# The last image's depthwise stage in another written-out order: TensorE's three parts first, VectorE's last part at the end

## The chip, the cores and the metric

The kernel runs on one NeuronCore of a Trainium2 chip. The metric is the device time of one execution in microseconds (us); smaller is better. All data are float32.

## The reference, cut to what matters

Four images of 256 channels and 64x64 pixels pass through four layers, each with a normalisation before it and a residual sum after it. The change touches only layer 2, and in it only the work of the last image: a small network generates, for each image, a 3x3 filter for every channel (`dk`) and a 256x256 mixing matrix (`pk`); the filters are applied channel by channel (depthwise), and the matrix mixes the channels (pointwise).

```python
def _gen_kernel(x, W1, b1, W2, b2):
    h = jax.nn.relu(jnp.einsum('bchw,rc->brhw', x, W1) + b1[None, :, None, None])
    pooled = h.mean(axis=(2, 3))
    return pooled @ W2.T + b2
B, C, H, W = x.shape
dk = _gen_kernel(x, Wd1, bd1, Wd2, bd2).reshape(B, C, K, K)
pk = _gen_kernel(x, Wp1, bp1, Wp2, bp2).reshape(B, O, C)
dw = lax.conv_general_dilated(x.reshape(1, B * C, H, W), dk.reshape(B * C, 1, K, K), (1, 1),
                              [(1, 1), (1, 1)], feature_group_count=B * C, ...).reshape(B, C, Ho, Wo)
out = jnp.einsum('bchw,boc->bohw', dw, pk) + bias[None, :, None, None]
...
x = x + _L2_conv_ref(_gn(x), ...)      # layer 2
x = x + _L3_conv_ref(_gn(x), ...)      # layer 3 follows
```

## The kernel before, in words

**Layout.** The 256 channels are two halves (`h` = 0 and 1, `NH` = 2) of 128 partitions; an image is `big[:, h, 4096 pixels]`. The normalised input of layer 2 lies in `xp` with a row of zeros above and below (`xin` is its inside). The depthwise result is made in eight parts: `PARTS` lists (c, h) for four stretches `c` of 1024 pixels and two channel halves, so part `2c + h` is half `h` of stretch `c`.

**Two ways to make a part.** On VectorE, ScalarE first writes the centre tap (`centre`, L1290), and then eight scalar_tensor_tensor instructions of 128x1024 add the other taps (`taps`, recorded at the helper's line L127). On TensorE, `taps_by_products` (matmul at L1339) multiplies the shifted input by nine diagonal matrices (`diag`, which ScalarE makes at L1352 from the filters of half 1). A part takes two PSUM banks of 512 columns, nine products each; after the ninth product ScalarE copies the bank to the part's tile (L1342). A float32 product appears in the trace as two matmul records. The images before the last make all eight parts on VectorE; only the last image has `diag`, because only there nothing of another image's attention is left for TensorE to do beside it.

**The mixing matrix.** `pk` starts as a bias and takes R = 8 scalar_tensor_tensor steps of 128x512, one for each slice of `wp2`. A DMA of SP's queue (`load_wp2`, L1223) brings two slices into one tile of the `k4` pool, so there are four loads.

**Pointwise.** For a stretch `c` and each 512 columns `s` of it, four products (two output halves `oh`, two input halves `h`, L1298) go to two PSUM banks; `pointwise_added` adds each bank to `big` on VectorE with a running sum (L1310), and ScalarE squares the result for the next layer's statistics (L1312). PSUM has eight banks of one pool, given out in turn (`bank`).

**Order.** The program is scheduled by hand: every engine executes its instructions in the order in which the Python code issues them, and a semaphore wait at an instruction holds what is behind it on the same engine. `Chain.later(n, f)` puts off a piece of work by n steps of the generator; `tick` runs what is due. `Chain.fill(n)` issues matmuls (L1444) of n pieces of the image before, which were kept in `held`; `Chain.settle()` issues their additions on VectorE (`res`, L127) and their stores (L1450, SP).

For the last image the order before the change is: VectorE makes the parts 0, 1, 2, 4, 6 (`mine`), TensorE the parts 3, 5, 7 (`others`). A credit lets TensorE's products in beside VectorE's taps, 54 products over 40 taps. After part 0 come `settle` and the eight steps of `pk`; two of the four slice loads are issued ahead, the other two after the second and the fourth step. The pointwise products of a stretch are put off by one and two steps after its last part on VectorE. `run(last)` runs this chain alone: no attention of another image is beside it.

The layer that follows (`mixed`) needs the sums of the whole image, so it begins with a wait for the last `pointwise_added`; its experts' load (L1390) is the next DMA in SP's order.

Of the kernel before, what the change touches and what calls it, by code (L numbers as in the profile page):

```python
# [10 lines left out]
ALU = mybir.AluOpType  # L11
# [3 lines left out]
NH = 2  # L15
HW = 64
N = HW * HW
CH = 1024
# [3 lines left out]
R = 8  # L22
# [71 lines left out]
def conv_preact_fast(ctx: ExitStack, tc: tile.TileContext, guard, x, wc, wtpg, ww, wqkv, wout, w1cat, wd2,  # L94
# [11 lines left out]
    def k4(name):  # L106
        return wk.tile([P, CH], F32, tag="k4", name=name, bufs=9)
# [3 lines left out]
    def k2(name):  # L111
        return wk.tile([P, 512], F32, tag="k2", name=name, bufs=5)
# [4 lines left out]
    def junk():  # L117
        return wk.tile([P, 512], F32, tag="junk", name="junk")

    def bank(name):  # L120
        return pp.tile([P, 512], F32, tag="bank", name=name, bufs=8)

    def tt(o, a, b, op):
        nc.vector.tensor_tensor(o, a, b, op)  # L124

    def stt(o, a, s, b, op0, op1):
        nc.vector.scalar_tensor_tensor(o, a, s, b, op0, op1)  # L127
# [119 lines left out]
    taps = wc_s.rearrange("p h (i j) o -> p h i (j o)", i=3)  # L247
# [950 lines left out]
    def generated(w, b, big, k4, st, sh, diag):  # L1198
# [19 lines left out]
        pk = k2("pk")  # L1218
        nc.sync.dma_start(out=pk, in_=bp2)

        def load_wp2(j):
            t = pool4("wp2").rearrange("p (r o) -> p r o", r=2)
            nc.sync.dma_start(out=t, in_=wp2[:, bass.ts(j, 2), :])  # L1223
            return t
# [12 lines left out]
        for c in range(N // 512):  # L1237
            if c < NC3:
                hidden(c)
            h, q = c % 2, c // 2  # L1240
# [17 lines left out]
        pb = sp.tile([P, 2 * R], F32, name="pb")  # L1258
# [25 lines left out]
        PARTS = [(c, h) for c in range(N // CH) for h in range(NH)]  # L1284

        def centre(i):
            c, h = PARTS[i]
            t = k4("dw")
            k = h * 9 + 4
            nc.scalar.activation(t.rearrange("p (y x) -> p y x", x=HW), xin[:, h, bass.ts(c, rows), :], AF.Copy, scale=dk[:, k:k + 1])  # L1290
            return t

        def pointwise(c, s, dw):
            res = []
            for oh in range(NH):
                ps = bank("ps_pw")
                for h in range(NH):
                    nc.tensor.matmul(ps, pk[:, h * NH * P + oh * P:h * NH * P + (oh + 1) * P], dw[h][:, bass.ts(s, 512)],  # L1298
                                     start=(h == 0), stop=(h == NH - 1))
                res.append(ps)  # L1300
            w.later(1, lambda: pointwise_added(2 * c + s, res))

        def pointwise_added(c, res):
            cols = bass.ts(c, 512)
            for oh in range(NH):
                if diag is None:
                    tt(big[:, oh, cols], res[oh], big[:, oh, cols], ALU.add)
                    nc.vector.bn_stats(st[:, oh, c, :], big[:, oh, cols])
                else:
                    nc.vector.scalar_tensor_tensor(big[:, oh, cols], res[oh], 1.0, big[:, oh, cols], ALU.mult, ALU.add,  # L1310
                                                   accum_out=sums[:, 0, oh, c:c + 1])
                    nc.scalar.activation(junk(), big[:, oh, cols], AF.Square, bias=pivot[:, oh:oh + 1],  # L1312
                                         accum_out=sums[:, 1, oh, c:c + 1])

        def taps(i):

            c, h = PARTS[i]
            dst = dw[i].rearrange("p (y x) -> p y x", x=HW)
            for ty, tx in TAPS:
                dx = tx - 1  # L1320
                x0, x1 = max(0, -dx), min(HW, HW - dx)
                k = h * 9 + 3 * ty + tx
                stt(dst[:, :, x0:x1], xp[:, h, c * rows + ty:c * rows + ty + rows, x0 + dx:x1 + dx], dk[:, k:k + 1],
                    dst[:, :, x0:x1], ALU.mult, ALU.add)
                yield 0.62

        def taps_by_products(parts):

            for i in parts:
                c, h = PARTS[i]  # L1330
                dw[i] = k4("dw")
                for s in range(2):
                    ps = bank("ps_dw")
                    dst = ps.rearrange("p (y x) -> p y x", x=HW)
                    for n, (ty, tx) in enumerate([(1, 1)] + TAPS):
                        dx = tx - 1
                        x0, x1 = max(0, -dx), min(HW, HW - dx)
                        y0 = (2 * c + s) * RB + ty
                        nc.tensor.matmul(dst[:, :, x0:x1], diag[:, 3 * ty + tx, :], xp[:, h, y0:y0 + RB, x0 + dx:x1 + dx],  # L1339
                                         start=(n == 0), stop=(n == 8))  # L1340
                        if n == 8:
                            nc.scalar.copy(dw[i][:, bass.ts(s, 512)], ps)  # L1342
                        yield


        mine = [i for i, (c, h) in enumerate(PARTS) if diag is None or h == 0 or c == 0]
        others = [i for i in range(len(PARTS)) if i not in mine]
        products, credit = taps_by_products(others), 0.0
        dw = {mine[0]: centre(mine[0])}
        if diag is not None:  # L1350
            for k in range(9):
                nc.scalar.activation(diag[:, k, :], ident, AF.Copy, scale=dk[:, 9 + k:10 + k])  # L1352
        slices = [load_wp2(0), load_wp2(1)]
        for n, i in enumerate(mine):
            if n + 1 < len(mine):
                dw[mine[n + 1]] = centre(mine[n + 1])
            for wait in taps(i):

                credit += 18 * len(others) / (8 * len(mine))
                while credit >= 1:  # L1360
                    credit -= 1
                    next(products, None)
                yield wait
            if n == 0:
                w.settle()
                for j in range(R):
                    stt(pk, slices[j // 2][:, j % 2, :], pb[:, R + j:R + j + 1], pk, ALU.mult, ALU.add)
                    if j % 2 == 1 and j // 2 + 2 < R // 2:
                        slices.append(load_wp2(j // 2 + 2))
                    yield 0.35  # L1370
            c, h = PARTS[i]
            if h == NH - 1 or i + 1 not in mine:
                if n == len(mine) - 1:
                    for _ in products:
                        pass
                d = [dw[2 * c + h] for h in range(NH)]
                for s in range(2):
                    w.later(1 + s, lambda c=c, s=s, d=d: pointwise(c, s, d))
        yield 2
        yield from w.pending()  # L1380
        sh2 = sp.tile([P, NH], F32, name="sh2")
        tt(sh2, sh, vec_s[:, V_L2B, :], ALU.add)
        return st, sh2
# [96 lines left out]
    def tail(b, big, qT, k4=k4, diag=None, xs_in=None, held=None):  # L1480

        def layers(w):
            st, sh = yield from nonlocal_out(w, b, big, k4, xs_in)
            st = yield from linear_attention(w, b, big, qT, k4, st, sh, diag is not None)
            st, sh = yield from generated(w, b, big, k4, st, sh, diag)
            if b + 2 < B:
                load_x(b + 2)
            elif b + 2 == B:
                for h in range(NH):
                    for q in range(2):  # L1490
                        half_image = bass.ts(q, N // 2)
                        nc.sync.dma_start(out=x_cols[:, h, half_image], in_=xs_d[b + 1, h, :, half_image])
            yield from mixed(w, b, big, k4, st, sh, held)
        return layers
# [23 lines left out]
    with tc.manual_schedule(engines={E.PE, E.Activation, E.DVE, E.Pool, E.SP}):  # L1518
# [15 lines left out]
        diag = tpg[:, NH, 0:9 * P].rearrange("p (k q) -> p k q", k=9)  # L1534
# [602 lines left out]
```

## Time and profile before

| what | value |
|---|---|
| median of 3 runs | 3113.34 us (3112.62 to 3114.3) |
| the profiled execution's own time | 3113.69 us |
| its span in the trace | 3111.8 us |
| busy: TensorE matmul, VectorE, ScalarE | 97%, 68%, 38% of the span |
| the last image's depthwise stage | 2974.6 us (first tap) to 3062.3 us (last sum) of the span |
| TensorE's work in it | 54 diagonal products and 32 pointwise products |
| VectorE's work in it | 40 taps, 8 steps of `pk`, 4 additions of `res`, 16 pointwise additions |

Times in the trace count from the span's start. "PE" is TensorE, "DVE" VectorE, "ACT" ScalarE, "SP" the engine that issues most DMAs. The shares over the whole span say little here: the change lies in a stage of 88 us, under 3% of the span, and has to be read from that stretch alone.

### The profile page before, as it was taken

How to read it: one execution, taken by the hardware profiler on the slowest of the kernel's cores; microseconds unless marked ns; L12 is line 12 of the kernel's file. 1: busy time of each engine (PE TensorE's matmuls, PEld its weight loads, DVE VectorE, ACT ScalarE, POOL GpSimd, SP SyncE). 2: the span in 40 equal slices, each digit the busy share in tenths (PEclk: the TensorE clock that was granted, in tenths of full speed). 3: DMA queues.
4: the chain of work that ended last, by engine and by line, in shares of the span. 5: the costliest groups of instructions: out<-in, count | busy, mean ns of one | idle time of the engine just before them, and what ended most of it. 6: DMA issues, size and time to landing. Idle time of an engine off the chain costs nothing.

```text
span 3111.8 us, 24418 instructions
## 1 busy us (share of the span) xinstructions
PE 3006.8 (97%) x8606; PEld 1486.8 (48%) x8606; DVE 2109.5 (68%) x2713; ACT 1174.0 (38%) x2188; POOL 131.1 (4%) x178
## 2 busy tenths in 40 slices
PE   6899999999999999999999999999999999998888
PEld 3454555445554444444565444444545544444633
DVE  8747777853557986786537896778363668864485
ACT  2134333353555322223364532222445443335621
POOL 0100000000110000000011000000100100000100
PEclk9999999999999999999999999999999999998999
DMA  5233111022101023113300102310420010111011
GB/s 217 77 105 137 35 51 30 31 55 85 40 11 34 7 75 125 39 43 63 109 11 1 41 21 82 107 46 29 102 75 1 11 34 14 44 49 63 14 61 65
DMA packets 58913, 174.25 MB, mean 56 GB/s; under 512 B 6432, under 2 KB 16416, under 8 KB 54560
## 3 DMA queue, kind: packets, MB, share of 16 engines
q1 hardware_dynamic: 54752, 155.85, 14.5%
q0 software_dynamic: 4032, 16.78, 2.9%
q8 instruction: 70, 1.15, 0.2%
q14 instruction: 59, 0.48, 0.1%
HBM read 111.26 MB, written 78.12 MB: 61 GB/s over the span
## 4 chain that ended last, share of the span: by engine, by line
PE 76%; DVE 17%; issue 5%; ACT 1%; DMA 0%; POOL 0%; POOLq 0%; SPq 0%; DVEq 0%; ACTq 0%
PE pf L898 22%; PE py L937 22%; PE ps_qkv L1057 5%; PE ps_conv L499 4%; DVE dw L127 4%; PE ps_tp L874 4%; PE ps_ex L1444 3%; DVE tot L124 3%; PE ps_pw L1298 3%; PE ps_conv L571 2%; PE ps_g L879 2%; PE ps_wy L921 2%; PE ps_o L1125 1%; DVE big L127 1%; DVE ra L127 1%
## 5 line engine op out<-in xcount | busy, mean ns | idle before, releaser
L899 ACT ACTIVATE pr<-pf 128x512 f32<-128x512 f32 x1024 | 603.6, 596 | 1183.8 <-PE pf L898 1138.1
L898 PE MATMUL pf<-tpg 128*128 128x512 f32 x2048 | 968.2, 595 | 2.9 <-ACT pr L899 2.9
L937 PE MATMUL py<-pr,tpg 128*128 128x512 f32 x2048 | 962.3, 592 | 2.5 <-ACT pr L899 2.3
L124 DVE TENSOR_TENSOR tot<-tot,pr 128x1024 f32<-128x1024 f32 x448 | 546.1, 1219 | 181.1 <-ACT pr L899 179.7
L937 PEld LDWEIGHTS py<-pr,tpg 128*128 128x128 f32 x2048 | 388.6, 190 | 494.4 <-issue 476.4
L898 PEld LDWEIGHTS pf<-tpg 128*128 128x128 f32 x2048 | 381.8, 190 | 438.4 <-issue 412.8
L127 DVE SCALAR_TENSOR_TENSOR dw<-xp,dk,dw 128x1008 f32<-128x1008 f32 x216 | 272.9, 1267 | 6.8 <-ACT dw L1290 3.7
L499 PE MATMUL ps_conv<-v,u 128*128 128x512 f32 x384 | 171.0, 593 | 3.6 <-DVE v L124 3.6
L1057 PE MATMUL ps_qkv<-wqkv_s,xg 128*128 128x384 f32 x384 | 129.9, 487 | 0.0
L124 DVE TENSOR_TENSOR tpg<-ps_g,bg_s 128x512 f32<-128x512 f32 x32 | 22.1, 691 | 144.4 <-PE ps_g L879 144.4
L874 PE MATMUL ps_tp<-big,wtpg_s 128*128 128x512 f32 x256 | 116.8, 599 | 3.0 <-ACT big L671 3.0
L499 PEld LDWEIGHTS ps_conv<-v,u 128*128 128x128 f32 x384 | 72.6, 190 | 96.5 <-issue 89.8
L217 POOL TENSOR_TENSOR rstd<-rstd,half 128x2 f32<-128x2 f32 x24 | 16.8, 701 | 2370.2 <-DVE rstd L354 2238.0
L1298 PE MATMUL ps_pw<-dw,pk 128*128 128x512 f32 x224 | 103.7, 597 | 8.7 <-DVE dw L127 8.7
L912 DVE RECIPROCAL inv<-pss 128x512 f32<-128x512 f32 x32 | 107.2, 3351 | 7.1 <-PE pss L910 7.1
L1057 PEld LDWEIGHTS ps_qkv<-wqkv_s,xg 128*128 128x128 f32 x384 | 72.2, 190 | 53.6 <-issue 9.3
L1067 DVE TENSOR_REDUCE qs<-qk 128x16 f32<-128x512 f32 x24 | 16.5, 686 | 118.6 <-ACT qk L1061 118.6
L875 ACT ACTIVATE tpg<-ps_tp,btp_s 128x512 f32<-128x512 f32 x64 | 43.7, 686 | 118.5 <-PE ps_tp L874 118.5
L874 PEld LDWEIGHTS ps_tp<-big,wtpg_s 128*128 128x128 f32 x256 | 47.5, 193 | 54.3 <-issue 49.8
L1127 ACT ACTIVATE junk<-ps_o 128x256 f32<-128x256 f32 x128 | 49.2, 385 | 63.7 <-PE ps_o L1125 59.4
L1298 PEld LDWEIGHTS ps_pw<-dw,pk 128*128 128x128 f32 x224 | 42.8, 192 | 63.1 <-issue 51.5
L1061 ACT ACTIVATE qk<-ps_qkv,rinv 128x256 f32<-128x256 f32 x96 | 45.5, 474 | 72.4 <-PE ps_qkv L1057 61.6
(339 smaller groups left out, 3147.2 us busy)
## 6 DMA issues: line engine op xcount, KB each, us to landing
xp<-in_x_dram SPq DMA_DIRECT2D x16, 1024.0 KB, 6.4
wy_d<-wt SPq DMA_DIRECT2D x32, 512.0 KB, 3.0
out_dram<-res SPq DMA_DIRECT2D x64, 256.0 KB, 2.0
wy<-wy_d SPq DMA_DIRECT2D x28, 512.0 KB, 4.6
xs_d<-big POOLq DMA_DIRECT2D x24, 512.0 KB, 11.0
u<-filters SPq DMA_DIRECT2D x48, 256.0 KB, 2.5
xs<-xs_d SPq DMA_DIRECT2D x24, 512.0 KB, 5.4
u<-rows_d SPq DMA_DIRECT2D x36, 256.0 KB, 3.1
```

The lines of the kernel that those rows point to most:

```text
L124: nc.vector.tensor_tensor(o, a, b, op)
L127: nc.vector.scalar_tensor_tensor(o, a, s, b, op0, op1)
L499: nc.tensor.matmul(ps[oh], u(oh, h), v[:, bass.ts(h, 512)], start=(h == 0), stop=(h == NH - 1))
L571: nc.tensor.matmul(ps[:, bass.ts(oh, IY * IX)], u[i][:, h, bass.ts(oh, P)], v[:, i, bass.ts(h, IY * IX)], start=(h == 0), stop=(h == NH - 1))
L874: nc.tensor.matmul(ps, wtpg_s[:, h, k, :], big[:, h, cols], start=(h == 0), stop=(h == NH - 1))
L898: nc.tensor.matmul(pf, phi[:, bass.ts(2 * m + s, P)], theta[:, bass.ts(q, 512)], start=True, stop=True)
L899: nc.scalar.activation(pr[:, bass.ts(s, 512)], pf, AF.Exp)
L912: nc.vector.reciprocal(inv, pss)
L937: nc.tensor.matmul(py, g[:, bass.ts(2 * m + s, P)], probs[i][:, bass.ts(s, 512)], start=(m == 0 and s == 0), stop=(m == NM - 1 and s == 1))
L1057: nc.tensor.matmul(ps[:, 0:3 * HID], xg[:, h, bass.ts(j, P)], wqkv_s[:, h, :], start=(h == 0), stop=(h == NH - 1))
L1298: nc.tensor.matmul(ps, pk[:, h * NH * P + oh * P:h * NH * P + (oh + 1) * P], dw[h][:, bass.ts(s, 512)], start=(h == 0), stop=(h == NH - 1))
L1444: nc.tensor.matmul(ps, wm[h][:, bass.ts(oh, P)], big[:, h, bass.ts(c, 512)], start=(h == 0), stop=(h == NH - 1))
```

## The change

The generator's middle part becomes two functions. `in_order` holds the order of the earlier images, with the same instructions in the same order (its `settle` is left out, and those chains hold nothing to settle). `shared_out` is the last image's order, written out by hand:

- TensorE makes the parts 1, 3, 5 (half 1 of the stretches 0, 1, 2), VectorE the parts 0, 2, 4, 6, 7. The number of parts on each engine is as before.
- All four slice loads are issued at the stage's beginning.
- The eight steps of `pk` are in two pieces of four, with three taps of part 2 between them.
- TensorE's order is: 24 diagonal products, pointwise of stretch 0 (8 products), 12 diagonal, stretch 1, 18 diagonal, stretch 2, stretch 3.
- VectorE's order is: part 0, `res`, four steps of `pk`, three taps of part 2, four steps of `pk`, five taps of part 2, then parts 4, 6 and 7 with the additions of the stretches 0 and 1 in fixed places between taps, and after part 7 the additions of the stretches 2 and 3.
- The centres of the parts 6 and 7 are issued on ScalarE after the additions (and squares) of stretch 0.

```diff
+        def pointwise_products(s, dw):
             ...
+            return res
+
+        def pointwise(c, s, dw):
+            res = pointwise_products(s, dw)
             w.later(1, lambda: pointwise_added(2 * c + s, res))
...
-        mine = [i for i, (c, h) in enumerate(PARTS) if diag is None or h == 0 or c == 0]
-        others = [i for i in range(len(PARTS)) if i not in mine]
-        products, credit = taps_by_products(others), 0.0
-        dw = {mine[0]: centre(mine[0])}
-        if diag is not None:
+        def mix_kernel(slices, js):
+
+            for j in js:
+                stt(pk, slices[j // 2][:, j % 2, :], pb[:, R + j:R + j + 1], pk, ALU.mult, ALU.add)
...
+        def shared_out():
+
+            slices = [load_wp2(j) for j in range(R // 2)]
+            yield from w.pending()
+            products = taps_by_products([2 * c + 1 for c in range(N // CH - 1)])
+            dw[0] = centre(0)
             for k in range(9):
                 nc.scalar.activation(diag[:, k, :], ident, AF.Copy, scale=dk[:, 9 + k:10 + k])
-        slices = [load_wp2(0), load_wp2(1)]
-        for n, i in enumerate(mine):
-            if n + 1 < len(mine):
-                dw[mine[n + 1]] = centre(mine[n + 1])
-            for wait in taps(i):
-
-                credit += 18 * len(others) / (8 * len(mine))
-                while credit >= 1:
-                    credit -= 1
-                    next(products, None)
-                yield wait
-            if n == 0:
-                w.settle()
-                for j in range(R):
-                    stt(pk, slices[j // 2][:, j % 2, :], pb[:, R + j:R + j + 1], pk, ALU.mult, ALU.add)
-                    if j % 2 == 1 and j // 2 + 2 < R // 2:
-                        slices.append(load_wp2(j // 2 + 2))
-                    yield 0.35
...
+            on_vector = {i: taps(i) for i in (0, 2, 4, 6, 7)}
+
+            def go(i, n):
+                for _ in range(n):
+                    next(on_vector[i])
+
+            def diagonal(n):
+                for _ in range(n):
+                    next(products)
+
+            def point(c):
                 d = [dw[2 * c + h] for h in range(NH)]
-                for s in range(2):
-                    w.later(1 + s, lambda c=c, s=s, d=d: pointwise(c, s, d))
-        yield 2
-        yield from w.pending()
+                return [(2 * c + s, pointwise_products(s, d)) for s in range(2)]
+
+            dw[2] = centre(2)
+            diagonal(24)
+            go(0, 8)
+            w.settle()
+            mix_kernel(slices, range(0, R // 2))
+            go(2, 3)
+            mix_kernel(slices, range(R // 2, R))
+            go(2, 5)
+            dw[4] = centre(4)
+            res = point(0)
+            diagonal(12)
+            pointwise_added(*res[0])
+            go(4, 1)
+            pointwise_added(*res[1])
+            go(4, 7)
+            dw[6], dw[7] = centre(6), centre(7)
+            res = point(1)
+            diagonal(18)
+            go(6, 1)
+            pointwise_added(*res[0])
+            go(6, 2)
+            pointwise_added(*res[1])
+            go(6, 5)
+            go(7, 8)
+            res = point(2)
+            pointwise_added(*res[0])
+            res = res[1:] + point(3)
+            for r in res:
+                pointwise_added(*r)
```

More of the change, by code (lines that the diff above doesn't have):

```diff
@@ L1291, in centre @@
             return t
-        def pointwise(c, s, dw):
+        def pointwise_products(s, dw):
             res = []
@@ L1343, in taps_by_products, with in_order @@
                         yield
-        mine = [i for i, (c, h) in enumerate(PARTS) if diag is None or h == 0 or c == 0]
-        others = [i for i in range(len(PARTS)) if i not in mine]
-        products, credit = taps_by_products(others), 0.0
-        dw = {mine[0]: centre(mine[0])}
-        if diag is not None:
+        def mix_kernel(slices, js):
+            for j in js:
+                stt(pk, slices[j // 2][:, j % 2, :], pb[:, R + j:R + j + 1], pk, ALU.mult, ALU.add)
+        dw = {}
+        def in_order(mine):
+            dw[mine[0]] = centre(mine[0])
+            slices = [load_wp2(0), load_wp2(1)]
+            for n, i in enumerate(mine):
+                if n + 1 < len(mine):
+                    dw[mine[n + 1]] = centre(mine[n + 1])
+                for wait in taps(i):
+                    yield wait
+                if n == 0:
+                    for j in range(R):
+                        mix_kernel(slices, [j])
+                        if j % 2 == 1 and j // 2 + 2 < R // 2:
+                            slices.append(load_wp2(j // 2 + 2))
+                        yield 0.35
+                c, h = PARTS[i]
+                if h == NH - 1:
+                    d = [dw[2 * c + h] for h in range(NH)]
+                    for s in range(2):
+                        w.later(1 + s, lambda c=c, s=s, d=d: pointwise(c, s, d))
+            yield 2
+            yield from w.pending()
@@ L1351, in generated @@
+        def shared_out():
+            slices = [load_wp2(j) for j in range(R // 2)]
+            yield from w.pending()
+            products = taps_by_products([2 * c + 1 for c in range(N // CH - 1)])
+            dw[0] = centre(0)
             for k in range(9):
                 nc.scalar.activation(diag[:, k, :], ident, AF.Copy, scale=dk[:, 9 + k:10 + k])
-        slices = [load_wp2(0), load_wp2(1)]
-        for n, i in enumerate(mine):
-            if n + 1 < len(mine):
-                dw[mine[n + 1]] = centre(mine[n + 1])
-            for wait in taps(i):
-                credit += 18 * len(others) / (8 * len(mine))
-                while credit >= 1:
-                    credit -= 1
-                    next(products, None)
-                yield wait
-            if n == 0:
-                w.settle()
-                for j in range(R):
-                    stt(pk, slices[j // 2][:, j % 2, :], pb[:, R + j:R + j + 1], pk, ALU.mult, ALU.add)
-                    if j % 2 == 1 and j // 2 + 2 < R // 2:
-                        slices.append(load_wp2(j // 2 + 2))
-                    yield 0.35
[L1371 to L1375, printed above, removed]
-                d = [dw[2 * c + h] for h in range(NH)]
-                for s in range(2):
-                    w.later(1 + s, lambda c=c, s=s, d=d: pointwise(c, s, d))
@@ L1381, in generated @@
+            go(6, 1)
[9 more added lines that the diff above has]
+                pointwise_added(*r)
+        if diag is None:
+            yield from in_order(range(len(PARTS)))
+        else:
+            yield from shared_out()
         sh2 = sp.tile([P, NH], F32, name="sh2")
```

## The prediction, made blind

> **What bounds the kernel now.** I began with the page's chain that ended last (PE 76% of the span), then asked for that chain in order of time over the last 150 us, because the change touches only the stage from 2974.6 to 3062.3 us. Its pieces (start, us, what):
>
> ```profile
> 3006.18 1.28 DVE dw L127
> 3007.46 0.04 issue
> 3007.50 4.58 PE ps_pw L1298 x6
> 3012.09 0.85 PE ps_dw L1339 x2
> 3012.93 3.43 PE ps_pw L1298 x8
> 3016.36 8.50 PE ps_dw L1339 x20
> ...
> 3054.74 6.88 PE ps_pw L1298 x16
> 3061.62 0.02 issue
> 3061.64 0.70 DVE tpg L1310 x2
> ```
>
> Up to 3007.46 the chain is VectorE: part 0, the additions of `res`, the mixing of `pk`, part 1. From 3007.50 it is TensorE without a break to 3061.62. So the end is set by TensorE after a late start. The waits over the stage (who <- for whom: total us, times, longest) and the stretches of it (us, busy of PE, PEld, DVE, ACT, POOL, granted clock, DMA share, GB/s) say why:
>
> ```profile
> DVE tpg L1310 <- PE ps_pw L1298: 13.7, 13, 3.2
> PE ps_pw L1298 <- DVE dw L127: 8.7, 1, 8.7
> DVE pk L127 <- DMA wp<-in_wp_dram: 3.3, 1, 3.3
> ```
> ```profile
> 2977.40:2997.80 20.40, 20.40 (x50) 9.13 (x49) 16.72 (x19) 4.12 (x5) 0.00 (x0) 1.00 0.48 154
> 2997.80:3007.50 9.70, 0.98 (x3) 0.15 (x1) 9.45 (x9) 0.00 (x0) 0.00 (x0) 0.65 0.00 0
> 3007.50:3061.60 54.10, 54.10 (x122) 23.74 (x122) 39.92 (x54) 15.39 (x35) 0.00 (x0) 0.97 0.00 0
> ```
>
> TensorE works through 24 diagonal products, then stands 8.72 us at the first pointwise product that reads part 1, which VectorE has not finished. The clock falls to half in that wait. VectorE later waits 13.7 us for products, which is free: TensorE is the bound there.
>
> [...] 0.50 from about 3000.8 to 3011.04, and the six records after the wait take 4.58 us. Full-speed records follow each other by 3.43/8 = 0.429 us, so six would take 2.57: the restart costs **2.0 us**. [...] two squares whose additions ended at 3015.9 and 3017.1 started at 3018.59 and 3019.43, behind the copy of a diagonal bank:
>
> ```profile
> 3018.11 0.59 ACT L1342 COPY rt<-ps_dw 128x512 f32<-128x512 f32 x1 [4.37 <-PE ps_dw L1339]
> 3018.59 0.72 ACT L1312 ACTIVATE junk<-tpg,pivot 128x512 f32<-128x512 f32 x1
> 3019.43 0.72 ACT L1312 ACTIVATE junk<-tpg,pivot 128x512 f32<-128x512 f32 x1
> ```
>
> **TensorE after the change.** The number of products stays. A pointwise product is two records, 0.858 us; a diagonal one 8.50/10 = 0.850. The first diagonal product starts at 2977.38 as before, behind the held pieces of the image before. Then, if no wait breaks in: 24 diagonal to 2997.8 (before, too, the 24 ended at 2997.76); stretch 0, 8 x 0.858, to 3004.6; 12 diagonal to 3014.8; stretch 1 to 3021.7; 18 diagonal to 3037.0; stretch 2 to 3043.9; stretch 3 to **3050.7**, against 3061.62. From the other side: 8.72 of wait and 2.0 of restart go, 10.7. I take **10.8**. What remains is whether each operand is there in time.
>
> **VectorE after the change.** A tap follows the last by 1.304 us (eight in 10.43), a step of `pk` by 0.76, the four `res` take 2.7, an addition 0.62 to 0.70. Part 0 ends at 2985.0, `res` at 2987.6, four steps at 2990.6, three taps of part 2 at 2994.5, four steps at **2997.6**. TensorE asks for `pk` at 2997.8: 0.2 us to spare. Five taps bring 3004.0, two additions (stretch 0's first products ended 3001.2) 3005.3, a tap 3006.6, two additions 3007.9, seven taps of part 4 3017.0. Now part 6 needs its centre, and here is the new wait. ScalarE's order is: copies of part 3 (the second waits for the 36th diagonal product, 3014.8, and starts about 0.2 later as now), four squares of about 0.8, then the centres of 6 and 7, 1.14 each. The copy starts at 3015.0, the squares at 3015.5, centre 6 at 3018.8, and it ends at 3019.9. **VectorE stands 2.9 us**; behind it are all its remaining taps. Then: tap, two additions, two taps, two additions, five taps to 3033.0 (centre 7 has been there since 3021.1); part 7's eight taps to **3043.4**. TensorE first reads part 7 with stretch 3's second product, at 3043.9 + 0.86 = 3044.7: 1.3 us to spare. The last four additions follow the products at 1.72 us, as they do now, and the last square too; the tail behind them is the same.
>
> **ScalarE and PSUM.** The copies of parts 1 and 5 stand ahead of the squares that could delay them, so stretch 2 finds part 5 copied by 3037.8, when its first product of half 1 is due at 3037.9. Counting banks in turn, each of stretches 1 to 3 takes banks emptied at least 5 us before (the tightest: stretch 2's first takes stretch 0's last, read by 3007.9). Cost: nothing. If an emptying were later than that, TensorE would wait one for one.
>
> **DMAs.** SP issues four slice loads from 2966.8 instead of two there and two at 2988.1; an issue costs 0.45, so until 2968.7. The pair at 2988.13 took 5.8 to land. Two pairs together should land between 5.8 and 2 x 5.8 us after 2968.7, by 2980.3. They are wanted at 2987.6 (slices 0, 1) and 2994.5 (2, 3). The cover is part 0 and `res`; without it each us late would stop TensorE one us, since the 12 diagonal products stand behind stretch 0 in its queue. SP's four `res` stores and the experts' load come behind the loads, as now, with 80 us until the experts are used. The 3.3 us wait of `pk` goes. Four loads hold four `k4` tiles at once; the transposes that last read tiles of that pool ended at 2955.
>
> **The earlier images.** `in_order` issues the same instructions in the same order: nothing, from -0.3 to +0.3 us.
>
> **The tail's clock.** After the stage TensorE is nearly idle for 7.7 us and `mixed` begins at half clock (0.50 until 3072.5: from 3069.34, 3.1 us, about 1.6 us lost). [...] I take +0.2.
>
> **Sum.** 3113.69 (span 3111.8 and 1.9 around it) - 10.8 + 0.2 = 3103.1 for a profiled execution. That one stood 0.35 over its median, so the median is **3102.7**, 0.34% faster. About 0.2%, 6.2 us, is what a measurement of this kernel can tell from no change.
>
> **The rivals.**
>
> *A, as worked out* (0.76): 3101 to 3104.5.
>
> *B, VectorE becomes the bound* (0.10). For it: the spare times are 0.2 us at `pk` and 1.3 at part 7, and the wait for centre 6 hangs on four squares. Against: each size is measured. Had VectorE 3 to 5 us more, the end would come 2 to 4 later: 3104.5 to 3106.7.
>
> *C, the order doesn't do what it says* (0.08): stretch 0's products, issued after part 2's last taps, also wait for those, until 3004.0. Then TensorE stands 6.2 us, and the clock falls again, 2.0: 3110.9, within 0.2%. Against: in the trace of before, the waiting product started 0.04 us after part 1's last tap while VectorE went on with taps, so waits go by instruction.
>
> *D, slower: the third and fourth slice come late*, because their tiles are given out only when a later reader frees them. SP then stands with the stores and loads behind it, VectorE at the fifth step, TensorE at stretch 0, and the diagonal products behind that can't fill the gap. With the restart's 2.0 it decides against the change from a stop of 8.8 us, slices landing after 3003.5; at 3010, 15.4 us stopped, the time is 3113.3 - 10.6 + 15.4 + 2.0 = 3120. Against: the third load before was released by SP's own store, not by a tile, and landed at 2993.9; even that is early enough here. 0.06.
>
> Faster takes A and B, 0.86; same C, 0.08; slower D, 0.06. The range runs from 3101 (no loss in the tail) to 3106.8, B's end; C and D, 0.14, lie outside.
>
> **What would show it.** Right: TensorE unbroken at clock 1.00 from 2977.4 to about 3050.7, no `pk` wait for `wp`, a wait of about 2.9 us of VectorE for centre 6, VectorE's last addition near 3051.5. Wrong: a wait of `ps_pw` for `pk` or `dw` over 1 us, or a clock of 0.50 inside the stage.

## The result and the profile after

The changed kernel takes **3104.12 us** (median of 7, 3101.91 to 3104.49) against 3114.43 (median of 7, 3112.62 to 3116.03) for the kernel before in the same rounds: 10.3 us less, a ratio of 0.9965 with a 95% interval from 0.9955 to 0.9974. Its profiled execution took 3104.24 us, with a span of 3102.5. TensorE's lines have moved: L1343 is the diagonal product, L1314 the pointwise addition, L1316 the square, L1346 the copy of a bank, L1498 the product of the last layer and the held pieces.

The chain of the kernel after, in order of time (start, us, what), from the first diagonal product to the end of the stage:

```profile
2978.40 20.39 PE ps_dw L1343 x48
2998.79 6.87 PE ps_pw L1298 x16
3005.65 10.19 PE ps_dw L1343 x24
3015.85 6.87 PE ps_pw L1298 x16
3022.71 15.29 PE ps_dw L1343 x36
3038.00 13.75 PE ps_pw L1298 x32
3051.75 0.02 issue
3051.77 0.70 DVE tpg L1314 x2
```

Between the first diagonal product and the last addition no VectorE instruction stands in it. The stretch view of the kernel after (us, busy of PE, PEld, DVE, ACT, POOL, granted clock, DMA share, GB/s) and its waits in the stage say the same: 73.4 us of TensorE without a gap, at full clock, and no wait of a product for `pk` or `dw`.

```profile
2977.40:3050.80 73.40, 73.40 (x174) 32.74 (x173) 66.29 (x81) 19.54 (x41) 0.00 (x0) 1.00 0.09 29
```
```profile
DVE tpg L1314 <- PE ps_pw L1298: 3.5, 4, 1.0
DVE dw L127 <- ACT dw L1290: 3.3, 1, 3.3
```

VectorE's waits for products fell from 13.7 to 3.5 us, its wait for the slices of `wp2` is gone, and there is one new wait of 3.3 us. Its place is seen in the timelines of ScalarE and VectorE (start, us, engine, line, operation, what, and in brackets the idle time before and its releaser):

```profile
3015.88 0.58 ACT L1346 COPY dw<-ps_dw 128x512 f32<-128x512 f32 x1 [7.06 <-PE ps_dw L1343]
3016.36 0.72 ACT L1316 ACTIVATE junk<-tpg,pivot 128x512 f32<-128x512 f32 x1
...
3018.90 0.72 ACT L1316 ACTIVATE junk<-tpg,pivot 128x512 f32<-128x512 f32 x1
3019.53 0.19 ACT L1316 ACTIVATION_READ_ACCUMULATOR junk<-tpg,pivot 128x1 f32 x1
3019.62 1.13 ACT L1290 ACTIVATE dw<-xp,dk 128x1024 f32<-128x1024 f32 x1
```
```profile
3008.34 9.12 DVE L127 SCALAR_TENSOR_TENSOR rt<-xp,dk,rt 128x1024 f32<-128x1024 f32 x7
3020.79 1.27 DVE L127 SCALAR_TENSOR_TENSOR dw<-xp,dk,dw 128x1008 f32<-128x1008 f32 x1 [3.33 <-ACT dw L1290]
```

Four squares, whose additions had ended by 3008.4, stood behind a copy that waited for TensorE; the centre of part 6 stood behind the squares, and VectorE behind the centre.

**Where the time went.** From the first diagonal product to the last pointwise one the stage took 84.24 us before (2977.38 to 3061.62) and 73.51 after (2978.24 to 3051.75): 10.73 less. (The chain above puts the first start at 2978.40, where the modelled end of the row before lies; 2978.24 is its own start in TensorE's timeline.) In these two executions the stage began 0.86 us later after the change, and what follows it took 50.75 us instead of 50.18. 10.73 - 0.86 - 0.57 = 9.30, the difference of the spans. The 0.57 comes from the first products after the stage, at half clock (0.50 until 3063.80, before until 3072.48): they took 0.73 more, and the rest of the tail 0.16 less. This is the chain of the kernel after (before, the same 20 records took 10.32):

```profile
3059.27 11.05 PE ps_ex L1498 x20
```

Of the 0.86 us, 0.23 were there at 261.9 us of the span, long before the stage. The rest does not look like chance: from the DMA there (SP, L648 `xs_d<-in_x_dram`) to the load of the last image's `pk` (SP, L1219) it is 2687.02 us in the kernel before and 2686.93 in e1, which has the old code too, but 2687.6 to 2687.8 in the changed kernel and in all nine kernels made from it. No run says why.

### The profile page after: what moved, and what is told of

It reads as the page before. It is cut to its first block, busy times and chain, and to the rows that moved or that the text cites. A ratio compares the mean times of both kernels' runs of the same rounds, so it can differ in the third digit from the quotient of the medians.

```text
span 3102.5 us, 24417 instructions
## 1 busy us (share of the span) xinstructions
PE 3005.3 (97%) x8606; PEld 1486.3 (48%) x8606; DVE 2108.8 (68%) x2713; ACT 1173.3 (38%) x2188; POOL 131.0 (4%) x178
## 4 chain that ended last, share of the span: by engine, by line
PE 77%; DVE 16%; issue 5%; ACT 1%; DMA 0%; POOL 0%; POOLq 0%; ACTq 0%; DVEq 0%; SPq 0%
PE pf L898 22%; PE py L937 22%; PE ps_qkv L1057 5%; PE ps_conv L499 4%; PE ps_tp L874 4%; DVE dw L127 4%; PE ps_ex L1498 3%; DVE tot L124 3%; PE ps_pw L1298 3%; PE ps_conv L571 2%; PE ps_g L879 2%; PE ps_wy L921 2%; PE ps_o L1125 1%; PE ps_dw L1343 1%; DVE big L127 1%
## 5 line engine op out<-in xcount | busy, mean ns | idle before, releaser
L127 DVE SCALAR_TENSOR_TENSOR dw<-xp,dk,dw 128x1008 f32<-128x1008 f32 x208 | 262.9, 1267 | 9.9 <-ACT dw L1290 7.0
L1298 PE MATMUL ps_pw<-dw,pk 128*128 128x512 f32 x224 | 101.3, 592 | 0.0
L124 DVE TENSOR_TENSOR v<-ra 128x1024 f32<-128x1024 f32 x58 | 69.5, 1219 | 0.4
```

## The experiments

Three questions were open: whether the gain is TensorE's wait and nothing else (theory M), whether the mixing and loads (R1) or the new share of parts (R2) bring it, and whether VectorE is really off the path (R3). Each kernel was timed with the kernel before in the same rounds; "difference" is that of the medians. The kernel before stood at 3113.85 us in the rounds of e1 to e4, at 3114.51 in those of e5 to e8 and at 3114.86 in those of e9 and e10, so across groups the differences compare better than the medians. The last column is the length of the stage in the one execution that was traced, from the first diagonal product to the last pointwise one; it holds neither the start nor the tail.

| run | median, us | difference | ratio to the kernel before (95%) | stage, us |
|---|---|---|---|---|
| kernel before | 3114.43 | | | 84.24 |
| changed kernel | 3104.12 | -10.3 | 0.9965 (0.9955 to 0.9974) | 73.51 |
| e1_put_off | 3102.98 | -10.9 | 0.9964 (0.9950 to 0.9977) | 73.50 |
| e2_parts_357 | 3104.98 | -8.9 | 0.9967 (0.9955 to 0.9979) | 73.50 |
| e3_pk_as_before | 3104.08 | -9.8 | 0.9966 (0.9952 to 0.9979) | 73.50 |
| e4_pk_late | 3113.59 | -0.3 | 0.9997 (0.9989 to 1.0006) | 82.06 |
| e5_18_ahead | 3110.91 | -3.6 | 0.9988 (0.9981 to 0.9994) | 80.28 |
| e6_centres_early | 3104.26 | -10.3 | 0.9966 (0.9954 to 0.9979) | 73.49 |
| e7_four_more | 3110.33 | -4.2 | 0.9986 (0.9979 to 0.9993) | 78.77 |
| e8_early_four_more | 3104.37 | -10.1 | 0.9966 (0.9953 to 0.9978) | 73.82 |
| e9_22_ahead | 3106.12 | -8.7 | 0.9973 (0.9962 to 0.9983) | 75.12 |
| e10_piece_in_gap | 3102.11 | -12.8 | 0.9958 (0.9944 to 0.9972) | 73.50 |

**e1: the kernel before, one number changed.**

```diff
-                    w.later(1 + s, lambda c=c, s=s, d=d: pointwise(c, s, d))
+                    w.later((1 if diag is None else 6) + s, lambda c=c, s=s, d=d: pointwise(c, s, d))
```

> The kernel before, with one number changed: in the last image the pointwise products are put off by 6 and 7 steps instead of 1 and 2; share of parts, mixing and loads as before. Theory M (the gain is the wait of TensorE at the first pointwise product plus the clock's restart, and it goes when enough diagonal products stand ahead): about 35 instead of 24 products stand ahead, they last until about 3007.7 and part 1 is ready at about 3008: no wait over 1 us, clock 1.00 in the stage, and the whole gain, 9 to 11 us under the kernel before (3103 to 3105). Rival R1 (the gain comes from the mixing in two pieces and the early loads, which take VectorE's 3.3 us wait away): nothing gained, 3113 to 3114. Rival R2 (it comes from the new share of parts): nothing gained, or at most half.

Measured: the whole gain. Its chain has no gap, and VectorE's wait for the slices is still there (from its waits):

```profile
2977.05 29.74 PE ps_dw L1339 x70
3006.79 3.43 PE ps_pw L1298 x8
3010.22 0.84 PE ps_dw L1339 x2
```
```profile
DVE pk L127 <- DMA wp<-in_wp_dram: 3.0, 1, 3.0
```

35 diagonal products (70 records) stand ahead of the first pointwise one instead of 24. Mixing, loads and share of parts are as before the change, so none of them is needed for the gain. This is the strongest evidence for M.

**e2: the changed kernel with the old share of parts.** VectorE's taps, centres and additions are moved to match; those lines are left out here.

```diff
-            products = taps_by_products([2 * c + 1 for c in range(N // CH - 1)])
+            products = taps_by_products([2 * c + 1 for c in range(1, N // CH)])
...
-            dw[2] = centre(2)
-            diagonal(24)
+            dw[1], dw[2], dw[4] = centre(1), centre(2), centre(4)
+            diagonal(36)
...
-            diagonal(12)
+            diagonal(9)
```

> The changed kernel with the share of parts as before: TensorE makes 3, 5, 7, VectorE 0, 1, 2, 4, 6; 36 diagonal products stand ahead of stretch 0, then 9 and 9 between the stretches; the centres are issued early. Theory M: part 1 is ready at about 3004.8, TensorE reaches stretch 0 at about 3008.8, so it never waits: the same time as the changed kernel within 1 us (3102.5 to 3105). R2: the gain is lost, in whole or by half (3108 to 3114). R1: as the changed kernel, since mixing and loads stay.

Measured: the same within the interval, and the stage is 73.50 us again. R2 falls: the share of parts is one way to have enough work ahead, and not the only one.

**e3: mixing and loads as before.**

```diff
-            slices = [load_wp2(j) for j in range(R // 2)]
+            slices = [load_wp2(0), load_wp2(1)]
...
-            mix_kernel(slices, range(0, R // 2))
-            go(2, 3)
-            mix_kernel(slices, range(R // 2, R))
-            go(2, 5)
+            for j in range(R):
+                mix_kernel(slices, [j])
+                if j % 2 == 1 and j // 2 + 2 < R // 2:
+                    slices.append(load_wp2(j // 2 + 2))
+            go(2, 8)
```

> The changed kernel with the eight steps of the mixing together and two of the four loads issued late, both as before. Theory M: the slices land at about 2994.8, VectorE waits about 3.3 us and has the matrix at about 2998, when TensorE asks for it at 2998.8; VectorE's lateness of 3 us then takes the place of its wait for the centre of part 6. The same time as the changed kernel within 0.5 us (3103 to 3104.5). R1: 3 us or more are lost, up to the whole gain (3107 to 3114).

Measured: no difference. The wait for the slices is back, and the wait for the centre of part 6 is gone from the list: the one took the place of the other, as expected.

```profile
DVE tpg L1314 <- PE ps_pw L1298: 3.5, 4, 1.0
DVE pk L127 <- DMA wp<-in_wp_dram: 3.2, 1, 3.2
```

So the two pieces and the early loads are worth nothing measurable here. R1 falls. They did not even bring the matrix sooner: in e3 it was ready at 2997.74, 19.63 us after the first diagonal product, and in the changed kernel at 2998.39, 20.15 after it, because the three taps between the two pieces (3.8 us) cost VectorE more than the 3.2 us of waiting that they replace.

**e4: the matrix late.** The second piece stands after all eight taps of part 2.

```diff
             mix_kernel(slices, range(0, R // 2))
-            go(2, 3)
+            go(2, 8)
             mix_kernel(slices, range(R // 2, R))
-            go(2, 5)
```

> The changed kernel with the second piece of the mixing after all eight taps of part 2 instead of three. The matrix is ready at about 3004.9, TensorE asks for it at 2998.8. Theory M (and the price that the prediction gave its case C): a wait of 6.1 us and a restart of the clock worth about 2.0: 8 us slower than the changed kernel (3111 to 3113). If a wait of this length did not lower the clock: 6 us (3109.5 to 3110.5). If TensorE's queue were not what sets the end: no difference.

Measured: the whole gain is lost. The timeline of TensorE:

```profile
3005.72 9.23 PE L1298 MATMUL ps_pw<-ra,pk 128*128 128x512 f32 x16 [6.20 <-DVE pk L127]
3014.79 10.36 PE L1343 MATMUL ps_dw<-xp,tpg 128*128 128x504 f32 x24
```

In the kernel after, the first of these rows is

```profile
2998.62 7.03 PE L1298 MATMUL ps_pw<-ra,pk 128*128 128x512 f32 x16
```

So e4 has a wait of 6.20 us, and then 16 records that take 2.20 more. The stage is 8.55 longer (82.06 instead of 73.51): the wait and 2.35 beyond it. The difference to the kernel before went from -10.3 to -0.3; the two traced executions are 10.2 apart, and what is not in the stage is a start 0.73 later and a tail 0.92 longer.

**e5 and e9: 18 and 22 products ahead instead of 24.**

```diff
-            diagonal(24)
+            diagonal(18)        # e9: 22
...
-            diagonal(12)
+            diagonal(18)        # e9: 14
```

> The changed kernel with 18 instead of 24 diagonal products ahead of stretch 0 (and 18 instead of 12 after it). TensorE asks for the mixing matrix at about 2993.7 and gets it at 2998.3. Theory M: a wait of 4.6 us, and on top of it 0 to 2 us[...]: 4.6 to 6.7 us slower than the changed kernel (3108 to 3111). R1 and R2 (mixing, loads and share of parts are all as in the changed kernel): no difference.

> The changed kernel with 22 instead of 24 diagonal products ahead of stretch 0 (and 14 instead of 12 after it). TensorE asks for the mixing matrix 1.7 us earlier, about 1.5 us before it is ready. Theory M: a wait of 1.4 to 1.6 us in the trace, and no fall of the clock, since in the earlier runs the clock fell at waits of 3.3 us and more[...]: 1.5 us slower than the changed kernel (3104.5 to 3106.5). If any wait lowers the clock: 3.5 us slower (3107 to 3108.5).

The first pointwise products of e5, then of e9, in TensorE's timeline:

```profile
2998.83 8.80 PE L1298 MATMUL ps_pw<-ra,pk 128*128 128x512 f32 x16 [4.85 <-DVE pk L127]
```
```profile
2999.07 7.13 PE L1298 MATMUL ps_pw<-ra,pk 128*128 128x512 f32 x16 [1.35 <-DVE pk L127]
```

e5's stage is 6.77 us longer than the changed kernel's, 4.85 of wait and 1.92 beyond it, as the medians have it (-3.6 instead of -10.3). e9 waits 1.35 and its clock stays at 1.00 through the stage, which is 1.61 longer, so 0.26 is lost beyond the wait without any fall of the clock. Its difference is -8.7 instead of -10.3; the intervals overlap, so for e9 the trace shows the loss and the times do not. Nothing differs among these kernels but how many of the first 36 products stand ahead of stretch 0, so that number is what the time follows.

**e6, e7, e8: VectorE's spare time.** e6 issues the centres of the parts 6 and 7 behind that of part 4; e7 does four taps of part 7 twice; e8 does both.

```diff
             dw[4] = centre(4)
+            dw[6], dw[7] = centre(6), centre(7)          # e6, e8
...
-            dw[6], dw[7] = centre(6), centre(7)          # e6, e8
...
             go(7, 8)
+            for _ in range(4):                           # e7, e8; more = taps(7)
+                next(more)
```

> The changed kernel with the centres of the parts 6 and 7 issued on ScalarE right after that of part 4, ahead of the squares. VectorE's wait of 3.3 us for the centre of part 6 goes. Theory M (TensorE is the bound from end to end): no difference in time, within 0.5 us; part 7 ends about 3 us earlier and VectorE waits for products instead. Rival R3 (VectorE is the bound, its order sets the end): about 3 us faster than the changed kernel (3100 to 3101).

> The changed kernel with four taps of part 7 done twice (the part then holds other values): 4 x 1.304 = 5.2 us more of VectorE ahead of stretch 3. In the changed kernel part 7 ended at 3043.7 and TensorE first read it at 3045.6, so 1.8 us are to spare. Theory M: 5.2 - 1.8 = 3.4 us slower than the changed kernel (3107 to 3108), as a wait of stretch 3's second product. R3: the whole 5.2 (3109).

> The changed kernel with the centres of the parts 6 and 7 early and four taps of part 7 done twice (the part then holds other values). Theory M: the 3.3 us of VectorE's wait for the centre and the 1.8 to spare nearly hold the 5.2 more: 0 to 1 us slower than the changed kernel (3103.5 to 3105). If the wait for the centre was no spare time: 3.4 us slower, as with the four taps alone.

e6 took VectorE's 3.3 us wait away and gained nothing: VectorE waits 6.5 us for products instead of 3.5. R3 falls. e8 put 5.2 us of work in that room for 0.3 us in the stage; so the wait was spare time indeed. e7 is the miss: 6.2 us above the changed kernel where 3.4 were expected. That is nearer to R3's 5.2, but e6 and e8 speak against R3, and the trace has another cause. TensorE's timeline and the clock of e7 show why:

```profile
3044.36 1.88 PE L1298 MATMUL ps_pw<-dw,pk 128*128 128x512 f32 x4
3049.55 1.12 PE L1298 MATMUL ps_pw<-rt,pk 128*128 128x512 f32 x2 [3.31 <-DVE rt L127]
3050.52 1.73 PE L1298 MATMUL ps_pw<-dw,pk 128*128 128x512 f32 x2
3052.04 1.91 PE L1298 MATMUL ps_pw<-rt,pk 128*128 128x512 f32 x2
```
```profile
3050.00:3050.50 0.50, 0.50 (x2) 0.19 (x1) 0.50 (x3) 0.30 (x1) 0.00 (x0) 1.00 0.00 0
3050.50:3051.00 0.50, 0.50 (x2) 0.19 (x1) 0.50 (x3) 0.50 (x2) 0.00 (x0) 0.69 0.00 0
3051.00:3052.00 1.00, 1.00 (x2) 0.34 (x1) 1.00 (x5) 0.93 (x4) 0.00 (x0) 0.50 0.00 0
```

The wait is 3.31 us, near the 3.4 worked out, but the clock fell too (1.00 until 3050.5, 0.50 from 3051.0), and only 1.1 us after the wait had ended. The stage is 5.26 us longer, the wait and 1.95 beyond it. The rest, again, lies in the start (0.51) and the tail (0.83).

**e10: one step further.** e6, and one held piece of the image before moved from behind layer 3's softmax to right behind the last pointwise product.

```diff
             for r in res:
                 pointwise_added(*r)
+            w.fill(1)
```

> The changed kernel with the centres of parts 6 and 7 early and one held piece of the image before (two products with their four records, 1.7 us) issued right behind the last pointwise product instead of after the softmax of layer 3. TensorE stands there 3.0 us now. Theory M (the tail's TensorE sets the end): the piece runs in that gap, the first product of the last layer starts up to 1.9 us earlier, and the time is 0.5 to 2 us under the changed kernel (3102 to 3103.5). Rival: the last layer's weights or the clock's later rise take the gain back, no difference.

The piece ran at 3051.71 to 3053.59, in the gap, and the row of held and first products after the softmax became shorter than the 11.05 above (L1499 is L1498 there; four records less):

```profile
3059.42 9.26 PE ps_ex L1499 x16
```

From the end of the last pointwise product to the first product with the new weights it is 13.2 us instead of 15.0. The eight held records of e10 from 3059.35 to 3065.08 took 2.30 us more than 8 x 0.429; the twelve of the kernel after, from 3059.20 to 3066.72, with the clock at 0.50 until 3063.80, took 2.37 more than 12 x 0.429. Both lost as much there, so the 1.8 us are not luck with the clock. The median is the lowest of all, but its interval overlaps the changed kernel's: the gain is shown by the trace, not by the times.

## Why the prediction was right

It gave 3102.7 us, in a range from 3101.0 to 3106.8, and 10.6 us under the median known then; measured are 3104.12 and 10.3. Most of the 1.4 between the two levels is the reference: with seven runs instead of three the kernel before stands 1.1 higher.

- **The bound.** TensorE's sum for the stage, gain 10.8: measured 10.73 in the two traced executions. The wait of 8.72 and the 2.0 beyond it are gone, as the stretch view with clock 1.00 shows, and e1, e4, e5 and e9 show that they are the cause.
- **The operands in time.** `pk` was ready at 2998.39, and the product that uses it began at 2998.62: 0.2 between, as predicted. But that 0.2 was not to spare. `pk` enters TensorE by a weight load ("PEld"), ahead of its product, which the prediction's sum left out. This is from the waits of the kernel after:

  ```profile
  PEld ps_pw L1298 <- DVE pk L127: 0.5, 1, 0.5
  ```

  The load began at 2998.44, 0.24 later than it would have without this wait, and takes 0.19 us, so it ended just as the product was due. Nothing was to spare, and that no time was lost was luck; with two products fewer ahead (e9) the wait was 1.35. The last copy of part 5 was as near: it ended at 3038.62, and its first reader began at 3038.70 (0.1 predicted).
- **The new wait** for the centre of part 6: 2.9 predicted, 3.3 measured. Its end came as worked out (3019.9 there, 3020.75 in an execution that began 0.86 later); VectorE reached it 0.4 earlier: it was 0.14 ahead at the first addition, the four additions took 0.61 each where the sum had 0.65, and the tap between them took 1.18 instead of 1.3. Further gains of this kind gave part 7 1.8 us to spare instead of 1.3. e6 and e8 show that the wait costs nothing.
- **The loads.** The four issues took 1.85 us from 2967.68 (4 x 0.45 predicted), each load landed within 6.9 us, by about 2976, and no wait for slices remains. e3 does not test the cover by part 0 and `res`: its late loads cost nothing because the three taps between the pieces are gone with them.
- **The earlier images.** Nothing was predicted, from -0.3 to +0.3 us; the kernels with the new code lose about 0.6 there, for a reason that stays open. It is the one term that lay outside its own limits.
- **The tail's clock.** 0.2 taken in the prediction, an estimate of the author's; 0.57 in this execution for the whole tail. The products after the stage ran at half clock (0.50) from 3059.20 to 3063.80 after the change, 4.6 us, where before it was 3.1 (3069.34 to 3072.48).
- **The rivals.** B's limit was 1.8 us away at part 7 (e7 crosses it). C's mechanism did not occur: the first pointwise product started at 2998.62, while the taps issued ahead of it ran on until 3004.8. Its price, 8.2 us, is confirmed by e4 at 8.55 in the stage. D did not occur; SP issued its four loads in a row.
- **What it did not say:** it took the change as a whole. Which part of it brings the gain was not split up. The new share of parts and the mixing in two pieces with early loads bring nothing measurable of themselves; what brings it is enough products ahead of stretch 0 to last until its operands are there.

## What to carry to other kernels

In an order written by hand, look for the first instruction on the bounding engine that reads another engine's result, and count the independent work ahead of it: here 24 products ahead left an 8.7 us hole and 35 left none, by one number. A wait on the engine that is not the bound is room, and could be filled here for next to nothing up to the next operand's due time: in e8 5.2 us of VectorE's work made the stage 0.3 longer. `pk`, which TensorE takes by a weight load, was due here when that load began (2998.44), not when the product did (2998.62). A wait of TensorE cost more than its length where the clock fell: here 1.9 to 2.4 us more in four traced executions.

## What the runs showed of the hardware

In the stage of four kernels TensorE's clock was at half (0.50) for a stretch during or after a wait, and in e9, with the shortest wait, it stayed at 1.00. Where it fell and rose is worked out from the clock in the stretch views. For the kernel before (columns as above; the third number from the end is the clock):

```profile
3000.00:3001.00 1.00, 0.00 (x0) 0.00 (x0) 0.96 (x2) 0.00 (x0) 0.00 (x0) 0.90 0.00 0
3010.50:3011.50 1.00, 1.00 (x3) 0.26 (x3) 1.00 (x2) 0.00 (x0) 0.00 (x0) 0.73 0.00 0
```

A mean of 0.90 over 1 us is 0.20 us at half clock, so the fall lies at 3000.80; 0.73 is 0.54 us, so the rise lies at 3011.04. In the same way for the others:

| run | TensorE's wait, us | from, to | clock 0.50 from, to | length, us | TensorE at work in it, us | lost beyond the wait, us |
|---|---|---|---|---|---|---|
| kernel before | 8.72 | 2998.78, 3007.50 | 3000.80, 3011.04 | 10.24 | 3.5 | 2.01 |
| e4 | 6.20 | 2999.52, 3005.72 | 3003.14, 3009.98 | 6.84 | 4.3 | 2.35 |
| e5 | 4.85 | 2993.98, 2998.83 | 2999.18, 3002.60 | 3.42 | 3.4 | 1.92 |
| e7 | 3.31 | 3046.24, 3049.55 | 3050.69, 3054.10 | 3.41 | 3.4 | 1.95 |
| e9 | 1.35 | 2997.72, 2999.07 | none | 0 | 0 | 0.26 |

The fall came 2.02, 3.62, 5.20 and 4.45 us after the wait had begun, in e5 and e7 when TensorE was at work again (for 0.35 and 1.14 us). So the length of a wait alone did not set the moment of the fall. These runs do not show what set it, and none of them has a wait between 1.35 and 3.31 us in the stage.

What a fall cost here follows from how long TensorE worked at half clock. Half of each of these times is 1.7 to 2.1, and with the 0.26 that e9 lost without a fall this makes 2.0, 2.4, 2.0 and 2.0, against the 2.01, 2.35, 1.92 and 1.95 measured beyond the waits. It was not one price: the 20 records behind the softmax of layer 3 worked at half clock for 3.14 us in the kernel before and for 4.60 in the kernel after, and took 10.32 and 11.05 us, 1.7 and 2.5 more than 20 x 0.429. In e9 they took 11.82 us, 3.2 more than 20 x 0.429; its clock there is not shown:

```profile
3061.73 11.82 PE ps_ex L1498 x20
```

On three engines a waiting instruction held those issued behind it: on TensorE for 8.72 us in the kernel before, with diagonal products behind the pointwise one; on ScalarE, where four squares of the kernel after stood behind the copy of 3015.88; on VectorE, where the taps stood 3.33 us behind the first tap of part 6.
